# A layer-normalized RWKV attention with a Hadamard feed-forward: a recurrence with fewer VectorE passes, an earlier normalization, and one more quarter product split into seven

## The chip, the cores and the metric

The kernel runs on one core of a Trainium2 chip. The metric is the time of one execution on the device, in microseconds (us). Five engines of the core work side by side, each through its own instructions in order: TensorE (PE in the profile; PEld are its weight loads), VectorE (DVE), ScalarE (ACT), GpSimd (POOL) and SyncE (SP), which here issues nearly all transfers. An engine that waits for another one holds up everything that is queued behind the waiting instruction.

## The reference, cut to what matters

The input x has 4 sequences of 2048 tokens with 512 channels. H is 2048 in the feed-forward.

```python
xn = (x - mean) / sqrt(var + 1e-5)            # over the channels
shifted = xn one token later, zero first
xr, xk, xv = mu * xn + (1 - mu) * shifted     # one mu each
r, k, v = xr @ Wr.T, xk @ Wk.T, xv @ Wv.T
# recurrence over the tokens, per channel; w_eff = -exp(w)
#   p  = max(pp, u + k);      e1  = exp(pp - p);          e2  = exp(u + k - p)
#   y  = (e1 * aa + e2 * v) / (e1 * bb + e2)
#   p2 = max(w_eff + pp, k);  e1b = exp(w_eff + pp - p2); e2b = exp(k - p2)
#   aa, bb, pp = e1b * aa + e2b * v, e1b * bb + e2b, p2
att = (sigmoid(r) * y) @ Wo.T
hidden = silu(xn @ W1.T) * (xn @ W3.T)
ffn = fwht(hidden) @ W2.T                     # Hadamard transform of size 2048, scaled
out = x + att + ffn
```

All is in 32-bit floats. Of two numbers a and b, max(a, b) can be had as b + relu(a - b), and exp(a - max(a, b)) as exp(-relu(b - a)).

## The kernel before

**Blocks and stages.** The tokens are taken in eight blocks of 1024 (i from 0 to 7, two a sequence). Each block has two big stages on TensorE. In the first stage it makes k, v and r (projections; `projected_pair`, L429, six units, from block 1 on) and the hidden units (`up`, L459, sixteen units j = 0 to 15). From block 1 on the order is unit j = 0, the six projections (two of k, two of v, two of r), then j = 1 to 15. In the second stage (`down`, L747; `down_whole`, L655, for block 0) one last product gives attention and feed-forward together: the Hadamard transform is folded into W2 in block 0, and Wo is stacked to it.

**Seven products for eight.** A unit (`seven`, L371) multiplies 2 x 2 quarters by seven products instead of eight. Its TensorE order is fixed: forms 0, 4, 5, then the left-over work of the unit before (`tail`), then forms 1, 3, 6, 2. Between them ScalarE copies partial sums from one PSUM bank to another, so that a later product adds onto them:

```python
product(pa, 0, m11, True)
act.copy(pb, pa)
product(pf, 4, f1, True)
act.copy(s5, pf)
product(pb, 5, f2, False)
```

The third product of a unit therefore starts only after the copy `pb <- pa` is done. After form 3 come `on22` and after form 6 `on12`, where VectorE finishes two quarters and then `step()` (or `hook()`) issues one piece of other work.

**The recurrence.** `wkv(h)` (L287) does one of four channel groups ("heads" here) of the recurrence as whole-row instructions of 128 x 1024 on tiles `sa`, `sb`, `e1`, `e1b`, cut by `yield` into nine pieces. The first piece is a max-scan into `sa` and one subtraction into `sb`; the exponentials are on ScalarE. From block 1 on, head 0 is worked off during the projections at fixed calls of `hook()` (5, 6, 8, 11 to 15, 17; there are three in a projection: `on11`, `on22`, `on12`), so its first two pieces fall on `on22` and `on12` of the second projection. Before the piece each `hook()` also advances the mixing of xn with its shifted copy and its quarter differences (`mix_chores`). The other heads get two pieces a unit from j = 1 on: head 1 starts in `on22` of j = 1, head 2 in `on12` of j = 5, head 3 in `on22` of j = 10. In block 0 the pieces start at j = 0.

**Order.** All engines' instructions stand in the order of the program text (`InOrder`, L25, which is why nearly all rows of the profile name L35). Nothing is moved by a scheduler.

**The last product.** `down` splits the product by quarters again: seven forms (0 to 6). Forms 1 to 6 are split into seven a second time (`Deep`, L706), each a `step` of five matmul pairs of 256 columns; form 0, the one on the first quarters, is left plain: four steps of five matmul pairs of 512 columns (`plain_step`). Every 32-bit matmul shows as two records. `Deep.forms` are VectorE differences of 128 x 1280. Weight pieces of 320 KB come through a ring of eight slots (`pieces_w`), seven ahead of their use. `deep_forms` makes the weights of the second split once, on GpSimd, in block 1.

**Chores in `down`.** While the last product of a block runs, ScalarE takes mean and variance of the next block's tokens (`statistics`: 16 pieces on `x_tok`, which lies in `tf`), GpSimd the inverse root, SP writes both to memory and reads them back spread over all partitions (`spread`, in `v_sb`), and VectorE normalizes the next block's channels (`normalize`, eight instructions of 128 x 1024) and takes their four differences (`token_forms`).

Of the kernel before, what the change touches and what calls it, by code (L numbers as in the profile page):

```python
# [40 lines left out]
def tile_rwkv_attn_hadamard_ffn(  # L41
# [37 lines left out]
    down_w = dram.tile([2, 7, KH, P, QR, P], F32, name="down_w")  # L79
    deep_w = dram.tile([6, 7, P, QR, P], F32, name="deep_w")  # L80
    stat_d = dram.tile([n_blocks, 2, TB], F32, name="stat_d")


# [57 lines left out]
    def load_tokens(i):  # L141
        sp.dma_start(out=x_tok, in_=x[ds(i * TB, TB), :].rearrange("(p t) c -> p t c", p=P))

    def load_channels(i, t0=0, n=TB):
        dst = xnT[:, :, OFF + t0 : OFF + t0 + n]
        sp.dma_start(out=dst, in_=xT[:, ds(i * TB + t0, n)].rearrange("(b p) t -> p b t", p=P))

# [15 lines left out]
    def statistics(i):  # L163

        sums = small.tile([P, 2, TP], F32, tag="sums", name=f"sums_{i}")
        rs = small.tile([P, 2, TP], F32, tag="rs", name=f"rs_{i}")
        mean = small.tile([P, TP], F32, tag="mean", name=f"mean_{i}")
        for t in range(TP):
            tok = x_tok[:, t, :]
            act.activation(tok, tok, AF.Copy, accum_out=sums[:, 0, t : t + 1])  # L170
            yield
        pool.tensor_scalar(mean, sums[:, 0, :], -1.0 / C, None, ALU.mult)
        for t in range(TP):
            tok = x_tok[:, t, :]
            act.activation(tok, tok, AF.Square, bias=mean[:, t : t + 1], accum_out=sums[:, 1, t : t + 1])
            if t + 1 < TP:
                yield
        pool.tensor_scalar(rs[:, 0, :], sums[:, 1, :], 1.0 / C, EPS, ALU.mult, ALU.add)
        pool.tensor_tensor(rs[:, 0, :], rs[:, 0, :], neg_half, ALU.pow)
        pool.tensor_tensor(rs[:, 1, :], mean, rs[:, 0, :], ALU.mult)  # L180
        sp.dma_start(out=stat_d[i].rearrange("s (p t) -> p s t", p=P), in_=rs)
        sp.dma_start(out=spread, in_=stat_d[i].unsqueeze(0).to_broadcast([P, 2, TB]))
        yield

    def token_before(i):
# [5 lines left out]
    def normalize():  # L191

        for b in range(NB):
            for s, op in ((0, ALU.mult), (1, ALU.add)):
                xb = xnT[:, b, OFF : OFF + TB]
                dve.tensor_tensor(xb, xb, spread[:, s, :], op)
                yield

# [87 lines left out]

    def wkv(h):  # L287
        w_h, u_h = weff[:, h : h + 1], vec[:, 4, h : h + 1]
# [4 lines left out]
        cy = [carry[:, h, n : n + 1] for n in range(3)]  # L293

        def exp(t):
            act.activation(t, t, AF.Exp)


        copy(first_a, cy[0])
        scan(a1, w_h.to_broadcast([P, TB]), k, first_a, ALU.add, ALU.max)  # L300
        tt(b1, k, a1, ALU.subtract)
        yield
        stt(e1b, a0, w_h, a1, ALU.add, ALU.subtract)
        stt(e1, k, u_h, a0, ALU.add, ALU.max)
        stt(k, k, u_h, e1, ALU.add, ALU.subtract)
        tt(e1, a0, e1, ALU.subtract)
        copy(cy[0], last_a)
        yield
        exp(b1)
        exp(e1b)  # L310
        yield

        copy(first_a, cy[1])
        tt(a1, b1, v, ALU.mult)
# [4 lines left out]
        exp(e1)  # L319
        yield  # L320
        copy(first_b, cy[2])
        scan(b1, e1b, b1, first_b, ALU.mult, ALU.add)
        copy(cy[2], last_b)
        tt(v, k, v, ALU.mult)
        yield
        num, den = e1, e1b
        tt(den, e1, b0, ALU.mult)
        tt(den, den, k, ALU.add)
        dve.reciprocal(den[:, 0:H], den[:, 0:H])
        yield  # L330
# [217 lines left out]
    PARTS = ((0, 0), (1, 0), (1, 1), (0, 1))  # L548
    DEEP = (1, 4, 6, 5, 2, 3)

# [13 lines left out]
    def plain(form):  # L564
        return [("plain", form, PARTS[n]) for n in (0, 1, 3, 2)]

    def deep(m, *which):
        return [("deep", m, n) for n in which]

    order = (0, 1, 4, 6, 5, 3, 2)  # L570
    whole_program = [p for form in order for p in plain(form)]
    p1 = plain(0)
    program = [p1[0], p1[1], *deep(0, 0, 1), p1[2], *deep(0, 2), p1[3], *deep(0, 3, 4, 5), *deep(1, 0), *deep(0, 6)]
    for m, *which in (
# [39 lines left out]
    class Down:  # L614
# [30 lines left out]

        def plain_step(self, form, g, rh, pts, y, start=False):
            self.product(("plain", form, (rh, g)), pts[g], quarter(*y, rh, whole), whole, start and rh == 0)

        def plain_product(self, form, pts, y, then, start=False):
            for g in range(KH):  # L650
                for rh in range(2):
                    self.plain_step(form, g, rh, pts, y, start)
                then(g)

    def down_whole(i, chores, next_parts):  # L655
# [8 lines left out]
        chores.start()  # L664
        chores.statistics(2 * TP)
        next_parts()
# [10 lines left out]
        for g in range(KH):  # L677
            add(x22[g], s5[g])
        chores.tokens(6)
        d.plain_product(6, pc, (1, 1), lambda g: None)  # L680
# [7 lines left out]
        d.residual(x21, 1, 0)  # L688
        chores.tokens(2)

        def c22(g):
            add(x22[g], pb[g])
            d.store(x22[g], 1, g, 1)

        d.plain_product(3, pb, (0, 1), c22)
        chores.tokens(4)
        chores.mix()
# [48 lines left out]

    def down(i, chores, next_parts, last):  # L747
        d = Down(i)
# [13 lines left out]
        s5 = [s[:, cols] for s in s5 for cols in (lo, hi)]  # L762
        d0 = Deep(d, 0, sets[0], y21, [*free, in_k[2]], s5[0])
        d1 = Deep(d, 1, sets[1], y11, [slot(v_flat), *in_k[0:2], in_tf[0]], s5[2])
        d2 = Deep(d, 2, sets[0], y22, [*free, in_tf[1]], s5[1])
# [21 lines left out]

        def first(g, rh):
            d.plain_step(0, g, rh, pa, (0, 0), True)

        def with_u2(g):
            for slots, mh, half in ((x12, 0, 1), (x22, 1, 1), (x21, 1, 0)):
                add(slots[g], u2_of[g])
                if slots is not x21:
                    d.store(slots[g], mh, g, half)

        d.residual(x11, 0, 0)
        d.residual(x12, 0, 1)
        d.residual(x22, 1, 1)
        d0.clear()  # L800
        d0.forms(0, 1, 2, 3)
        first(0, 0)
        first(0, 1)
        d1.clear()
        chores.start()
        add(x11[0], pa[0])
        d0.step(0, 1)
        first(1, 0)
        chores.statistics(4)
        t1(0, 1)  # L810
        d1.forms(0)
        d0.step(2)
        chores.statistics(2)
        t3(0, 1)
        first(1, 1)
        chores.statistics(4)
        add(x11[1], pa[1])
        for g in range(KH):
            act.copy(u2_of[g], pa[g])
        t1(2, 3)  # L820
        d1.forms(1)
        d0.step(3)
        chores.statistics(1)
        d0.step(4)
        chores.statistics(2)
        d0.onto(0, x11)
        d1.forms(2, 3)
        d0.step(5)
        chores.statistics(1)
        d1.step(0)  # L830
        d0.step(6)
        chores.statistics(1)
        t3(2, 3)
# [4 lines left out]
        d1.step(1)  # L838
        chores.statistics(1)
        d5.step(0)  # L840
# [17 lines left out]
        d2.step(1)  # L858
        chores.tokens(3)
        d5.step(2)  # L860
        d1.step(5)
        d2.step(2)
        chores.tokens(2)
        d5.step(3)
# [29 lines left out]
        d4.forms(2)  # L894
        chores.tokens(2)
        d3.step(4)
# [6 lines left out]
        d3.step(5)  # L903
        chores.tokens(5)
        d4.step(5)
# [46 lines left out]
    class Chores:  # L952


        def __init__(self, i):
            self.i = i
            self.of_statistics, self.of_tokens = statistics(i), chain(normalize(), token_forms(dve))

# [4 lines left out]

        def do(self, pieces, n):
            if self.i < n_blocks:
                for _ in range(n):
                    next(pieces)

        def statistics(self, n):
            self.do(self.of_statistics, n)  # L970

        def tokens(self, n):
            self.do(self.of_tokens, n)

# [5 lines left out]
    for i in range(n_blocks):  # L980
# [5 lines left out]

        pieces = (None for h in range(NB) for _ in wkv(h))

# [81 lines left out]
        for j in range(0 if i == 0 else 1, NF):  # L1070
            w = group(j if i == 0 else 3 * KH + j)
            if i == 0 and j <= NR:
                if j > 1:
                    keep_down()
                if j < NR:
                    t = down_parts(0) if j == 0 else t_next
                    keep_down = down_forms(j, folded, t)
                    if j == 0:
                        keep_down()
                    t_next = down_parts(j + 1) if j + 1 < NR else None  # L1080
            if i == 1 and j in (3, 5, 7, 9, 11, 13):
                keep_deep(j // 2 - 1, t)
# [5 lines left out]
            tail = up(i, j, w, tail, step)  # L1088
        for f in tail:
            f()  # L1090
        for _ in pieces:
            pass


        def next_parts():
            if not last:
                parts.extend(load_parts(i + 1, n) for n in order_of(i + 1)[:2])

        if not last:
            load_tokens(i + 1)  # L1100
        if i == 0:
            down_whole(i, Chores(i + 1), next_parts)
        else:
            down(i, Chores(i + 1), next_parts, last)

# [52 lines left out]
```

## Time and profile before

| what | us |
|---|---|
| median of 3 runs (3043.6 to 3043.85) | 3043.84 |
| the profiled execution, its own time | 3040.92 |
| its span, first to last instruction | 3039.1 |
| TensorE busy | 3024.6 (100%) |
| VectorE busy | 2470.7 (81%) |
| ScalarE busy | 1015.1 (33%) |
| GpSimd busy | 232.3 (8%) |
| transfers, share of 16 engines (largest queue) | 37.9% |

An engine's busy time is the union of its instructions. TensorE's instructions overlap and their ends are modelled, so its busy share alone doesn't say that it never waits; the distance from one matmul's start to the next does. In a row of the timeline the first number is the start, the second how long the merged instructions take, x the number of instructions, and in brackets is the idle time ahead of it with the engine that ended it. The mean granted clock of TensorE is 0.999 of full speed.

### The profile page before, as it was taken

Reading aid. Unit: us, or ns where it says so; the run is one execution under the profiler, and the core shown is the slowest. Engines: PE = TensorE matmul, PEld = TensorE weight load, DVE = VectorE, ACT = ScalarE, POOL = GpSimd, SP = SyncE. Lnnn points to the kernel's source line nnn. Section 1 sums busy time; section 2 is a strip of 40 time slices with the busy share of each in tenths; the row PEclk is TensorE's granted clock in tenths of the full one; section 3 lists DMA queues with packets and bytes.
Section 4 is the critical chain, followed back from the end, with each engine's and each line's share of the span. In section 5 each row is a group of like instructions: output and inputs, shape, how many; then the busy total and the mean of one; then the engine's idle time right before and its main releaser. Section 6 shows DMA issues by size and latency. Waiting matters only on the chain.

```text
span 3039.1 us, 24405 instructions
## 1 busy us (share of the span) xinstructions
PE 3024.6 (100%) x8492; PEld 1613.1 (53%) x8492; DVE 2470.7 (81%) x2579; ACT 1015.1 (33%) x1822; POOL 232.3 (8%) x192
## 2 busy tenths in 40 slices
PE   8999999999999999999999999999999999999999
PEld 3444444447644476444854448544485445844458
DVE  7798648897888888888887878789798887988877
ACT  4233124332243323433233332433324333143321
POOL 3263002320000000000000000000000000000000
PEclk9999999999999999999999999999999999999999
DMA  4264523666422263222632236322453224522234
GB/s 175 76 213 160 190 90 128 216 215 221 133 82 76 79 235 132 73 78 100 226 119 82 73 130 203 113 74 84 159 169 118 73 73 170 180 95 85 73 115 151
DMA packets 136058, 397.64 MB, mean 131 GB/s; under 512 B 14336, under 2 KB 32768, under 8 KB 133760
## 3 DMA queue, kind: packets, MB, share of 16 engines
q1 hardware_dynamic: 135648, 395.50, 37.9%
q8 instruction: 68, 1.11, 0.1%
q10 hardware_dynamic: 288, 0.59, 0.1%
q14 instruction: 54, 0.44, 0.0%
HBM read 336.08 MB, written 59.96 MB: 130 GB/s over the span
## 4 chain that ended last, share of the span: by engine, by line
PE 96%; DVE 2%; DMA 1%; POOL 0%; ACT 0%; issue 0%; POOLq 0%; SPq 0%; ACTq 0%; DVEq 0%
PE bank L35 96%; DMA pieces_w<-deep_w 1%; POOL rs L35 0%; DVE right L35 0%; DVE e1b L35 0%; DMA right<-w 0%; DVE e L35 0%; DVE v_sb L35 0%; DMA stat_d<-rs 0%; DVE sb L35 0%; DVE bank L35 0%; DVE sa L35 0%; ACT tf L35 0%; DVE xnT L35 0%; POOLq L1154 0%
## 5 line engine op out<-in xcount | busy, mean ns | idle before, releaser
L35 PE MATMUL bank<-tf,part 128*128 128x512 f32 x2048 | 941.5, 592 | 0.0
L35 ACT COPY bank<-bank 128x512 f32<-128x512 f32 (+1 forms) x638 | 337.1, 528 | 1413.7 <-PE bank L35 1383.2
L35 PE MATMUL bank<-right,pieces_w 128*128 128x256 f32 (+1 forms) x2928 | 789.3, 429 | 0.4 <-DMA pieces_w<-deep_w 0.2
L35 PE MATMUL bank<-xnT,part 128*128 128x512 f32 x1536 | 722.0, 592 | 0.7 <-DVE right L35 0.7
L35 PEld LDWEIGHTS bank<-right,pieces_w 128*128 128x128 f32 x2928 | 555.9, 190 | 227.2 <-issue 166.7
L35 PEld LDWEIGHTS bank<-tf,part 128*128 128x128 f32 x2048 | 389.1, 190 | 489.8 <-issue 461.6
L35 PEld LDWEIGHTS bank<-xnT,part 128*128 128x128 f32 x1536 | 291.6, 190 | 366.4 <-issue 358.9
L35 DVE TENSOR_TENSOR right<-right 128x1280 f32<-128x1280 f32 (+2 forms) x236 | 327.7, 1414 | 63.4 <-PE bank L35 62.4
L35 PE MATMUL bank<-right,part 128*128 128x512 f32 x840 | 369.6, 593 | 0.0
L35 DVE SCALAR_TENSOR_TENSOR right<-right,bank 128x512 f32<-128x512 f32 x256 | 174.5, 682 | 223.3 <-ACT right L35 223.1
L35 PEld LDWEIGHTS bank<-right,part 128*128 128x128 f32 x840 | 158.4, 190 | 203.2 <-issue 189.4
L35 ACT ACTIVATE right<-bank 128x512 f32<-128x512 f32 x308 | 184.6, 600 | 130.1 <-PE bank L35 111.0
L35 DVE RECIPROCAL e1b<-e1b 128x512 f32<-128x512 f32 x64 | 214.1, 3347 | 1.1
L35 DVE TENSOR_TENSOR bank<-bank,s 128x512 f32<-128x512 f32 x256 | 168.7, 690 | 37.3 <-ACT bank L35 23.7
L35 DVE TENSOR_TENSOR right<-right,bank 128x512 f32<-128x512 f32 x256 | 173.5, 678 | 11.5 <-PE bank L35 7.1
L35 POOL TENSOR_SCALAR mean<-sums 128x8 f32<-128x8 f32 x7 | 5.8, 835 | 1869.6 <-ACT tf L35 1869.6
L35 DVE SCALAR_TENSOR_TENSOR right<-xnT,vec,right 128x1024 f32<-128x1024 f32 x92 | 121.5, 1357 | 7.9 <-ACT right L35 7.9
L35 ACT COPY s<-bank 128x512 f32<-128x512 f32 x128 | 75.0, 586 | 145.4 <-PE bank L35 145.4
L35 POOL TENSOR_TENSOR part<-part 128x256 f32<-128x256 f32 x88 | 89.1, 1023 | 203.9 <-DMA part<-wpart 96.9
L35 ACT ACTIVATE right<-xnT,omm 128x1024 f32<-128x1024 f32 x92 | 100.3, 1141 | 12.3 <-PE bank L35 12.3
L35 PE MATMUL bank<-pieces_w,part 128*128 128x512 f32 x224 | 100.7, 592 | 0.0
L35 PE MATMUL bank<-k_sb,pieces_w 128*128 128x256 f32 x420 | 97.5, 379 | 0.0
(120 smaller groups left out, 2299.8 us busy)
## 6 DMA issues: line engine op xcount, KB each, us to landing
part<-part_w SPq DMA_DIRECT2D x148, 896.0 KB, 4.6
pieces_w<-deep_w SPq DMA_DIRECT2D x294, 320.0 KB, 3.1
pieces_w<-down_w SPq DMA_DIRECT2D x80, 320.0 KB, 5.5
part_w<-part SPq DMA_DIRECT2D x22, 896.0 KB, 6.0
tf<-x SPq DMA_DIRECT2D x7, 2048.0 KB, 8.1
xnT<-xT SPq DMA_DIRECT2D x7, 2048.0 KB, 10.0
deep_w<-pieces_w SPq DMA_DIRECT2D x6, 2240.0 KB, 9.3
v_sb<-xT SPq DMA_DIRECT2D x48, 256.0 KB, 8.2
```

The costliest lines, as they stand in the source:

```text
L35: return self.tc.keep_in_program_order(issue(*args, **kwargs))
```

## The change

Three things are changed.

- **Recurrence.** The maxima and subtractions ahead of the exponentials are replaced by one signed difference, its two one-sided parts (`Relu` with scale 1 or -1 on ScalarE) and exponentials with scale -1. Per head three VectorE passes go and four ScalarE passes come. The first two `Relu` are in the second piece and read what the first piece leaves in `sb`.
- **Normalization.** For blocks 3 to 7 the channels are normalized one block earlier, during the hidden units of the block before: `normalize_early` uses `pieces_w` as scratch, and the result goes through a buffer in memory (`xn_d`). The token statistics move one block earlier too; block 0's last product does two sets.
- **Last product.** From block 1 on, form 0 is split into seven as well (`d6`), its steps alternating with those of the split form of the next one (`d0`). Its weights are made in block 0 at j = 12 and kept at j = 14.

```diff
-    deep_w = dram.tile([6, 7, P, QR, P], F32, name="deep_w")
+    deep_w = dram.tile([7, 7, P, QR, P], F32, name="deep_w")
+    xn_d = dram.tile([C, TB], F32, name="xn_d")
...
+    def normalize_early(i):
+        flat = pieces_w.rearrange("p u q c -> p (u q c)")
+        both = flat[:, 0 : 2 * TB].rearrange("p (s t) -> p s t", t=TB)
+        slots = [flat[:, ds((2 + n) * TB, TB)] for n in range(3)]
+        def load(b):
+            sp.dma_start(out=slots[b % 3], in_=xT[ts(b, P), ds(i * TB, TB)])
+        load_spread(i, both)
+        for b in range(3):
+            load(b)
+        yield
+        for b in range(NB):
+            xb = slots[b % 3]
+            for s, op in ((0, ALU.mult), (1, ALU.add)):
+                dve.tensor_tensor(xb, xb, both[:, s, :], op)
+                if s:
+                    sp.dma_start(out=xn_d[ts(b, P), :], in_=xb)
+                    if b + 3 < NB:
+                        load(b + 3)
+                yield
...
-    def wkv(h):
+    def wkv(h, ahead):
+        def below(out, t, sign):
+            act.activation(out, t, AF.Relu, scale=-sign)
         def exp(t):
-            act.activation(t, t, AF.Exp)
+            act.activation(t, t, AF.Exp, scale=-1.0)
         scan(a1, w_h.to_broadcast([P, TB]), k, first_a, ALU.add, ALU.max)
-        tt(b1, k, a1, ALU.subtract)
-        yield
-        stt(e1b, a0, w_h, a1, ALU.add, ALU.subtract)
-        stt(e1, k, u_h, a0, ALU.add, ALU.max)
-        stt(k, k, u_h, e1, ALU.add, ALU.subtract)
-        tt(e1, a0, e1, ALU.subtract)
+        stt(b1, a0, w_h, k, ALU.add, ALU.subtract)
         copy(cy[0], last_a)
         yield
+        below(e1b, b1, 1.0)
+        below(b1, b1, -1.0)
+        stt(e1, k, u_h, a0, ALU.add, ALU.subtract)
+        ahead(1)
+        yield
+        exp(e1b)
         exp(b1)
-        exp(e1b)
+        ahead(2)
         yield
+        below(k, e1, 1.0)
+        below(e1, e1, -1.0)
...
-    DEEP = (1, 4, 6, 5, 2, 3)
+    DEEP = (1, 4, 6, 5, 2, 3, 0)
...
-    program = [p1[0], p1[1], *deep(0, 0, 1), p1[2], *deep(0, 2), p1[3], *deep(0, 3, 4, 5), *deep(1, 0), *deep(0, 6)]
+    program = [p for n in (0, 4, 1, 2, 3, 5) for p in (*deep(6, n), *deep(0, n))]
+    program += [*deep(1, 0), *deep(6, 6), *deep(0, 6)]
...
+        d6 = Deep(d, 6, (*pa, sets[1][2]), y11, [*in_k, in_k[1]], s5[3])
...
-        d0.forms(0, 1, 2, 3)
-        first(0, 0)
-        first(0, 1)
...
+        d6.step(0)
+        d6.clear("f")
+        d0.clear("f")
+        d6.forms(0)
+        d0.step(0)
+        d0.forms(0)
+        d6.step(4)
+        d6.forms(1)
...
+            if j == 1:
+                ahead(1)
+            if i == 0 and j == NR + 2:
+                t = deep_forms(6)
+            if i == 0 and j == NR + 4:
+                keep_deep(6, t)
```

More of the change, by code (lines that the diff above doesn't have):

```diff
@@ L142, in load_tokens @@
         sp.dma_start(out=x_tok, in_=x[ds(i * TB, TB), :].rearrange("(p t) c -> p t c", p=P))
+    FIRST_EARLY = 3
     def load_channels(i, t0=0, n=TB):
         dst = xnT[:, :, OFF + t0 : OFF + t0 + n]
+        if i >= FIRST_EARLY:
+            sp.dma_start(out=dst, in_=xn_d.rearrange("(b p) t -> p b t", p=P))
+            return
         sp.dma_start(out=dst, in_=xT[:, ds(i * TB + t0, n)].rearrange("(b p) t -> p b t", p=P))
@@ L181, in statistics, with load_spread @@
         sp.dma_start(out=stat_d[i].rearrange("s (p t) -> p s t", p=P), in_=rs)
-        sp.dma_start(out=spread, in_=stat_d[i].unsqueeze(0).to_broadcast([P, 2, TB]))
         yield
+    def load_spread(i, out):
+        sp.dma_start(out=out, in_=stat_d[i].unsqueeze(0).to_broadcast([P, 2, TB]))
     def token_before(i):
@@ L319, in wkv @@
         exp(e1)
-        yield
         copy(first_b, cy[2])
@@ L323, in wkv @@
         copy(cy[2], last_b)
-        tt(v, k, v, ALU.mult)
         yield
         num, den = e1, e1b
+        tt(v, k, v, ALU.mult)
         tt(den, e1, b0, ALU.mult)
         tt(den, den, k, ALU.add)
+        yield
         dve.reciprocal(den[:, 0:H], den[:, 0:H])
@@ L571, in tile_rwkv_attn_hadamard_ffn @@
     whole_program = [p for form in order for p in plain(form)]
-    p1 = plain(0)
-    program = [p1[0], p1[1], *deep(0, 0, 1), p1[2], *deep(0, 2), p1[3], *deep(0, 3, 4, 5), *deep(1, 0), *deep(0, 6)]
+    program = [p for n in (0, 4, 1, 2, 3, 5) for p in (*deep(6, n), *deep(0, n))]
+    program += [*deep(1, 0), *deep(6, 6), *deep(0, 6)]
     for m, *which in (
@@ L644, in matmuls @@
                 )
-        def plain_step(self, form, g, rh, pts, y, start=False):
-            self.product(("plain", form, (rh, g)), pts[g], quarter(*y, rh, whole), whole, start and rh == 0)
         def plain_product(self, form, pts, y, then, start=False):
@@ L651, in plain_product @@
                 for rh in range(2):
-                    self.plain_step(form, g, rh, pts, y, start)
+                    rows = quarter(*y, rh, whole)
+                    self.product(("plain", form, (rh, g)), pts[g], rows, whole, start and rh == 0)
                 then(g)
@@ L664, in down_whole @@
         chores.start()
-        chores.statistics(2 * TP)
+        chores.statistics(2 * TP + 1)
         next_parts()
@@ L678, in down_whole @@
             add(x22[g], s5[g])
-        chores.tokens(6)
+        chores.normalize(6)
+        chores.statistics(1)
         d.plain_product(6, pc, (1, 1), lambda g: None)
@@ L688, in down_whole @@
         d.residual(x21, 1, 0)
-        chores.tokens(2)
+        chores.normalize(2)
+        chores.statistics(TP)
         def c22(g):
@@ L693, in c22 @@
             d.store(x22[g], 1, g, 1)
+        chores.statistics(TP - 1)
         d.plain_product(3, pb, (0, 1), c22)
-        chores.tokens(4)
+        chores.statistics(1)
+        chores.forms(4)
         chores.mix()
@@ L745, in onto, with down @@
                         dve.tensor_tensor(slot[g][:, hi], slot[g][:, hi], self.s5, ALU.add)
-    def down(i, chores, next_parts, last):
+    def down(i, chores, next_parts, last, before):
         d = Down(i)
@@ L762, in down @@
         s5 = [s[:, cols] for s in s5 for cols in (lo, hi)]
-        d0 = Deep(d, 0, sets[0], y21, [*free, in_k[2]], s5[0])
-        d1 = Deep(d, 1, sets[1], y11, [slot(v_flat), *in_k[0:2], in_tf[0]], s5[2])
+        d6 = Deep(d, 6, (*pa, sets[1][2]), y11, [*in_k, in_k[1]], s5[3])
+        d0 = Deep(d, 0, sets[0], y21, [*free, free[1]], s5[0])
+        d1 = Deep(d, 1, sets[1], y11, [slot(v_flat), in_k[0], in_k[2], in_tf[0]], s5[2])
         d2 = Deep(d, 2, sets[0], y22, [*free, in_tf[1]], s5[1])
@@ L786, in t4, with first_u2 @@
             sums(y21, y21, y22, *which)
-        def first(g, rh):
-            d.plain_step(0, g, rh, pa, (0, 0), True)
+        def first_u2(g):
+            u, pt = u2_of[g], (d6.a, d6.b)[g]
+            act.copy(u[:, lo], pt[:, lo])
+            dve.tensor_tensor(u[:, hi], pt[:, hi], d6.s5, ALU.add)
+            add(x11[g], u)
         def with_u2(g):
@@ L795, in with_u2 @@
                     d.store(slots[g], mh, g, half)
-        d.residual(x11, 0, 0)
-        d.residual(x12, 0, 1)
-        d.residual(x22, 1, 1)
-        d0.clear()
-        d0.forms(0, 1, 2, 3)
-        first(0, 0)
-        first(0, 1)
[L804 to L822, printed above, removed]
+        d6.clear("a")
+        d0.clear("a")
+        before()
+        d6.step(0)
[6 more added lines that the diff above has]
+        d6.forms(1)
+        d.residual(x11, 0, 0)
+        d0.step(4)
+        d0.forms(1)
+        d6.step(1)
+        d6.forms(2)
+        d0.step(1)
+        chores.statistics(2)
+        d6.step(2)
+        d6.forms(3)
+        d0.forms(2)
+        chores.statistics(2)
+        d0.step(2)
+        d0.forms(3)
+        t1(0)
+        chores.statistics(2)
+        d6.step(3)
+        t1(1)
+        chores.statistics(2)
+        d0.step(3)
+        d1.forms(0)
+        first_u2(0)
+        d1.clear()
+        chores.statistics(2)
+        d6.step(5)
+        t1(2, 3)
+        d.residual(x12, 0, 1)
         chores.statistics(1)
-        d0.step(4)
-        chores.statistics(2)
+        d0.step(5)
         d0.onto(0, x11)
-        d1.forms(2, 3)
-        d0.step(5)
         chores.statistics(1)
         d1.step(0)
+        d1.forms(1)
+        d.residual(x22, 1, 1)
+        chores.statistics(1)
+        d6.step(6)
+        t3(0, 1)
+        chores.statistics(1)
         d0.step(6)
-        chores.statistics(1)
+        chores.start()
+        d1.forms(2, 3)
+        first_u2(1)
         t3(2, 3)
@@ L838, in down @@
         d1.step(1)
-        chores.statistics(1)
+        chores.statistics(3)
         d5.step(0)
@@ L858, in down @@
         d2.step(1)
-        chores.tokens(3)
+        chores.normalize(3)
         d5.step(2)
@@ L862, in down @@
         d2.step(2)
-        chores.tokens(2)
+        chores.normalize(2)
         d5.step(3)
@@ L894, in down @@
         d4.forms(2)
-        chores.tokens(2)
+        chores.normalize(2)
         d3.step(4)
@@ L903, in down @@
         d3.step(5)
-        chores.tokens(5)
+        chores.normalize(1)
+        chores.forms(4)
         d4.step(5)
@@ L956, in __init__, with all_statistics @@
             self.i = i
-            self.of_statistics, self.of_tokens = statistics(i), chain(normalize(), token_forms(dve))
+            self.of_statistics = self.all_statistics()
+            self.of_normalize = iter(()) if i >= FIRST_EARLY else normalize()
+            self.of_forms = token_forms(dve) if i < n_blocks else iter(())
+        def all_statistics(self):
+            if self.i == 1:
+                yield from statistics(1)
+                load_spread(1, spread)
+                load_tokens(2)
+                yield
+            if self.i + 1 < n_blocks:
+                yield from statistics(self.i + 1)
+            if self.i == 2:
+                load_spread(2, spread)
+                yield
         def start(self):
@@ L962, in start, with normalize, forms @@
                 load_channels(self.i)
[L964 to L967, printed above, removed]
         def statistics(self, n):
-            self.do(self.of_statistics, n)
-        def tokens(self, n):
-            self.do(self.of_tokens, n)
+            for _ in range(n):
+                next(self.of_statistics, None)
+        def normalize(self, n):
+            for _ in range(n):
+                next(self.of_normalize, None)
+        def forms(self, n):
+            for _ in range(n):
+                next(self.of_forms, None)
         def mix(self):
@@ L984, in tile_rwkv_attn_hadamard_ffn, with ahead @@
             dve.memset(carry[:, :, 1:3], 0.0)
-        pieces = (None for h in range(NB) for _ in wkv(h))
+        early = normalize_early(i + 1) if FIRST_EARLY <= i + 1 < n_blocks else None
+        def ahead(n):
+            for _ in range(n if early else 0):
+                next(early, None)
+        pieces = (None for h in range(NB) for _ in wkv(h, ahead if h else lambda n: None))
         def step():
@@ L1088, in tile_rwkv_attn_hadamard_ffn, with before @@
             tail = up(i, j, w, tail, step)
[L1089 to L1092, printed above, removed]
+        def before():
+            for f in tail:
+                f()
+            for _ in pieces:
+                pass
+            if i == 0:
+                load_tokens(1)
+            elif i + 2 < n_blocks:
+                load_tokens(i + 2)
         def next_parts():
@@ L1097, in next_parts @@
                 parts.extend(load_parts(i + 1, n) for n in order_of(i + 1)[:2])
-        if not last:
-            load_tokens(i + 1)
         if i == 0:
+            before()
             down_whole(i, Chores(i + 1), next_parts)
         else:
-            down(i, Chores(i + 1), next_parts, last)
+            down(i, Chores(i + 1), next_parts, last, before)
 def kernel(**inputs):
```

## The prediction

> **What bounds the kernel now.** I read the page first: its busy times and its chain of waits.
>
> ```profile
> PE 3024.6 (100%) x8492; PEld 1613.1 (53%) x8492; DVE 2470.7 (81%) x2579; ACT 1015.1 (33%) x1822; POOL 232.3 (8%) x192
> PE 96%; DVE 2%; DMA 1%; POOL 0%; ACT 0%; issue 0%; POOLq 0%; SPq 0%; ACTq 0%; DVEq 0%
> ```
>
> TensorE is the bound, with no slack: matmul records outside the split forms start every 0.43 us, and after the first 23 us the starts fall behind that spacing by 2.4 us in all (1.25 in block 1, behind VectorE; 1.15 in three later blocks, where weight pieces queue on SP behind the statistics' store). So the time changes by TensorE work saved, less every new stall. VectorE's and ScalarE's busy times matter only where TensorE waits for them.
>
> **The split of form 0.** TensorE's timeline, block 0's unsplit last product and then split steps in block 4 (start, duration, x records):
>
> ```profile
> 305.90 120.33 PE L35 MATMUL bank<-right,pieces_w 128*128 128x512 f32 x280
> 1850.39 13.11 PE L35 MATMUL bank<-right,pieces_w 128*128 128x256 f32 x60
> 1863.35 2.32 PE L35 MATMUL bank<-tf,pieces_w 128*128 128x256 f32 x10
> ```
>
> The row after the first starts at 426.06: a 512-column record costs 120.16/280 = 0.429 us. From the other two, a 256-column one costs 12.96/60 = 0.216. Plain form 0 is 20 matmuls, 40 records, 17.17 us; split it is 7 x 5 matmuls, 70 records, 15.12. Saved: 2.05 a block, **14.3 us** in blocks 1 to 7. Making its weights lies on GpSimd, busy 8%: nothing.
>
> In exchange VectorE must make the forms of `d6` and `d0` early. Laid on the step times with 1.41 us for a 128 x 1280 subtraction, its queue is latest at the third difference of the third split form: ready 38.4 us into the stage, needed after 18 steps of 2.158, at 38.84. That fits with 0.4 us, because in blocks 2 to 6 the normalization no longer stands in `down`; everything else there has over 2 us. Below that margin it costs nothing, beyond it the lateness itself: 0 to 1.5 us a block; I take 0, the rows' own arithmetic.
>
> **Fewer VectorE passes, statistics earlier.** Three passes of some 1.3 us less a head, and 8 of 1.22 moved into the hidden units: VectorE isn't the bound there, so no gain. The moved loads (channels, spread) and stores (`xn_d`) are issued in unit j = 1 and used some 15 us later; like rows land in 5.4 us (spread) and 8.2 (256 KB of channels), so I take 0 (0 to 1 a block). The same 2 MB of channels then come from `xn_d` instead of x. Where the statistics' store no longer waits ahead of weight pieces, 1.15 us of stalls go, and block 1's 1.25 goes with the lighter VectorE: **2.4 us** gained (0 to 2.4).
>
> Block 0 takes two sets of statistics. The second 2 MB load enters SP's queue behind the spread, where four weight and mixing loads follow (340.8 to 342.9). The windows view shows 348 and 404 GB/s moved there already, so 2 MB take about 5.1 us, and the twelfth weight piece, landed at 349.3 and needed at 353.1, comes 1.3 late: **1.3 us** lost (0 to 3).
>
> **The first two `Relu`.** This decides. In `wkv`'s second piece ScalarE must wait for `sb`, which VectorE's first piece makes directly before. In ScalarE's order both `Relu` stand ahead of the next projection's copy `pb <- pa`, and that copy releases form 5 on TensorE. Head 0, block 4, timelines of VectorE, ScalarE and TensorE:
>
> ```profile
> 1580.45 2.35 DVE L35 TENSOR_TENSOR_SCAN sa<-weff,sa,k_sb 128x1024 f32<-128x1024 f32 x1
> 1582.90 1.23 DVE L35 TENSOR_TENSOR sb<-k_sb,sa 128x1024 f32<-128x1024 f32 x1
> ```
> ```profile
> 1583.06 0.57 ACT L35 COPY bank<-bank 128x512 f32<-128x512 f32 x1 [4.63 <-PE bank L35]
> ```
> ```profile
> 1582.81 3.60 PE L35 MATMUL bank<-pieces_w,part 128*128 128x512 f32 x8
> 1586.24 4.03 PE L35 MATMUL bank<-right,part 128*128 128x512 f32 x9
> ```
>
> The copy ran at 1583.06, as soon as form 0 was done. The TensorE row at 1582.81 is form 4 (four records) and then form 5, so form 5 starts at 1582.81 + 4 x 0.429 = 1584.53. After the change `sb` is a two-input pass with a scalar (1.28 instead of 1.23) and ready at about 1584.2. No row shows `Relu`. The nearest, exponentials of the same size on ScalarE:
>
> ```profile
> L35 ACT ACTIVATE sb<-sb 128x1024 f32<-128x1024 f32 x32 | 33.8, 1056 | 0.0
> ```
>
> Two of these end at 1586.3 (scaled copies of 1.14: 1586.5). The copy ends 0.57 later, and form 5 starts at 1586.9 instead of 1584.5: TensorE stands for **2.35 us** (2.2 to 2.6), once a block from block 1 on, 7 x 2.35 = **16.5** (15.4 to 18.2). Nothing makes it up, since TensorE has no slack.
>
> The same pair stands in the hidden units for heads 1 to 3. In blocks 2 to 7 head 1's first piece starts early enough: `Relu` and copy are over at 1644.5, needed at 1644.7, a margin of 0.2; I take 0 (0 to 0.5 each). In block 1 GpSimd makes the split weights, and VectorE's same instructions take longer beside it:
>
> ```profile
> 519.17 3.20 DVE L35 TENSOR_TENSOR_SCAN sa<-weff,sa,k_sb 128x1024 f32<-128x1024 f32 x1
> 522.40 2.38 DVE L35 TENSOR_TENSOR sb<-k_sb,sa 128x1024 f32<-128x1024 f32 x1
> ```
>
> That is 2.0 us later than in block 4, less the 0.2: **1.85** for head 1. Head 3, with a margin of 0.4, loses about **1.2** (0 to 2), and block 0's head 2 **0.2**.
>
> The Trainium skill ("ScalarE: Activation LUTs", "Rules for kernel authors") says that relu belongs on VectorE. By time alone the rows here disagree: 1.06 on ScalarE for 128 x 1024 in 32 bits, 1.22 to 1.28 on VectorE.
>
> **The sum without the clock.** 16.5 + 1.85 + 1.2 + 1.3 + 0.2 = 21.0 lost, 14.3 + 2.4 = 16.7 won: +4.3 us.
>
> **The clock.** The one long wait for VectorE in the trace, 2.76 us ahead of the matmul at 19.36, was followed by a halved clock; a shorter one at the end was not. Windows (length, busy time of PE, then of other engines; after POOL the granted clock):
>
> ```profile
> 15.50:18.90 3.40, 1.10 (x3) 0.19 (x1) 2.92 (x5) 0.96 (x3) 0.00 (x0) 1.00 1.03 386
> 18.90:22.30 3.40, 2.94 (x4) 1.39 (x5) 3.33 (x6) 1.22 (x2) 0.00 (x0) 0.51 1.05 395
> 3033.00:3036.30 3.30, 2.32 (x11) 1.71 (x9) 3.23 (x7) 0.00 (x0) 0.00 (x0) 1.00 0.47 179
> 3036.30:3039.10 2.80, 0.00 (x0) 0.00 (x0) 0.08 (x1) 0.00 (x0) 0.00 (x0) 1.00 0.47 163
> ```
>
> So a window with 32% of busy time was followed by half the clock, one with 70% was not. A stall of 2.35 us leaves 31% of such a window busy if it lies inside, and about 65% if it is cut in two. With the limit anywhere between 32% and 70%, about 5 of the 7 stalls fall below it, and each then costs half a window, 1.7 us: **+8.5** (0 to 7 x 1.7 = 11.9).
>
> By the Trainium skill ("TensorE: Matmul & The Clock Gate", "HAM oscillation") only idle gaps over about 3.4 us throttle again. The gap of 2.76 us above did, so I go by the row; by the page's rule the clock would stay and the time be 8.5 us less.
>
> **The sum.** 4.3 + 8.5 = +12.8 us. The profiled execution took 3040.92, so the changed one gives 3053.7. The median of the runs lies 2.92 above the profiled execution; I keep that: **3056.5 us**.
>
> **Rivals.**
> - *The stalls come, the clock holds.* For it: no gap after the start is longer than 0.73 us, so nothing shows what 2.35 does. The sum is +4.3 (2 to 7.5): 3048.1, or 3046 to 3051.
> - *The wait is covered* (the other side: not slower). If the first two `Relu` were done by the time form 4 ends, the 16.5 + 3.25 of the `Relu` and the clock's loss are away, and -16.7 + 1.3 = -15.4 is left; less 7 x 0.5 for thin margins, about -12: 3031.8 (3028 to 3036). It decides only if `sb` is ready 2.35 us earlier, by about 1581.85. VectorE's idle time of 5.2 us ahead of 1578.46 speaks for it, but that wait is for TensorE's products, from which the scan's `k` comes; scan and subtraction alone are 3.6 us. Also possible if the sums of TensorE's rows hide slack that I don't see.
> - *More than the stalls.* `Relu` takes turns with `Exp` eight times a block; one table load stands in the trace, at 1.28 us. If each turn loaded, 5 us of ScalarE a block would partly stretch the stalls, or `down`'s margin of 0.4 is missed by 1 to 2 us a block: +20 to +36, 3064 to 3080. Against it: the one load in the whole trace although exponentials and other functions already alternate.
>
> **How the numbers follow.** Clock falls: 0.50 (+8 to +20, 3051 to 3064). Clock holds: 0.28. Covered: 0.13. More than the stalls: 0.09. A measurement of this kernel can tell about 0.2% from no change, 6.1 us: "same" runs from 3037.8 to 3049.9. About a third of the second case lies beyond it, 0.09, as do all of the first and the last: slower 0.50 + 0.09 + 0.09 = 0.68; same 0.19; faster 0.13. The range leaves out the covered case and the far end of the last: 3045 to 3066.
>
> **What the profile after would show.** Right: TensorE idle once a projection stage, some 2.3 us, released by a ScalarE copy behind two `sb` activations of about 1.05 us that wait for VectorE; 280 fewer 512-column records in `down` and 490 more of 256 columns; stages of `down` shorter by 2; granted clock below 1.0 in a window behind each stall. Wrong: no gap there, or the clock at 1.00 right behind it, or gaps in `down` released by VectorE.

## The result, and the profile after

| | median, us | executions | lowest to highest |
|---|---|---|---|
| before | 3043.6 | 5 | 3040.7 to 3043.85 |
| after | 3052.48 | 5 | 3051.91 to 3058.63 |

The changed kernel is slower: ratio 1.0038, 95% interval 1.0023 to 1.0052. The profiled execution took 3052.48 against 3040.92 before, 11.6 us more (spans 3050.7 and 3039.1); the forecast for it was 12.8 more. By medians the loss is 8.9, because three of the five executions of before lay near 3043.8, 2.9 above the profiled one.

The page of the kernel after, busy times and chain:

```profile
PE 3014.0 (99%) x8702; PEld 1653.5 (54%) x8702; DVE 2391.1 (78%) x2525; ACT 1153.9 (38%) x1992; POOL 213.7 (7%) x196
...
PE 95%; DVE 3%; ACT 1%; DMA 1%; issue 0%; POOL 0%; SPq 0%; DVEq 0%; ACTq 0%; POOLq 0%
```

TensorE has 10.6 us less to do and VectorE 80 us less, and yet the span is longer: TensorE now stands. ScalarE is in the chain with 1%, where it had 0%. The waits view of TensorE (wait, total us, times, longest) names the engine:

```profile
PE bank L35 <- ACT bank L35: 18.3, 8, 3.4
...
PE bank L35 <- POOL part L35: 2.3, 1, 2.3
PE bank L35 <- DMA pieces_w<-down_w: 1.6, 1, 1.6
```

None of these three stood there before. The 2.3 us that the view puts down to GpSimd are the same stall in block 1: the two `Relu` and the copy stand ahead of it there too, and in the runs without `Relu` on ScalarE (e4, e5, e7 below) TensorE never waits for GpSimd. The place is the predicted one. Head 0 in block 4, timelines of VectorE, ScalarE and TensorE:

```profile
1589.26 2.35 DVE L35 TENSOR_TENSOR_SCAN sa<-weff,sa,k_sb 128x1024 f32<-128x1024 f32 x1
1591.71 1.28 DVE L35 SCALAR_TENSOR_TENSOR sb<-sa,weff,k_sb 128x1024 f32<-128x1024 f32 x1
```
```profile
1593.03 1.06 ACT L35 ACTIVATE e1b<-sb 128x1024 f32<-128x1024 f32 x1 [5.80 <-DVE sb L35]
1594.12 1.06 ACT L35 ACTIVATE sb<-sb 128x1024 f32<-128x1024 f32 x1
1595.08 0.58 ACT L35 COPY bank<-bank 128x512 f32<-128x512 f32 x1
```
```profile
1591.62 1.88 PE L35 MATMUL bank<-pieces_w,part 128*128 128x512 f32 x4
1595.72 1.98 PE L35 MATMUL bank<-pieces_w,part 128*128 128x512 f32 x4 [2.22 <-ACT bank L35]
```

ScalarE sits idle for 5.8 us until `sb` is there, does the two `Relu` of 1.06, and only then the copy. Form 4's four records start at 1591.62 and are through at 1591.62 + 4 x 0.429 = 1593.34; form 5 starts at 1595.72, 2.38 us late (the bracket shows less because the ends of matmuls are modelled).

**Where the 11.6 us are.** From TensorE's starts: seven such stalls, 7 x 2.38 = 16.7; head 1 of block 1, 1.7; head 3 of block 1, 3.6; the weight piece in block 0, 1.7; three stretches of halved clock, 1.7 + 1.7 + 1.5 = 4.9 (the rows follow). Lost: 28.6. Won: the last product takes 105.76 instead of 107.82 (block 3), 7 x 2.06 = 14.4, the waits for `deep_w` pieces 1.2, and a stretch of halved clock in the first 25 us, 1.8, that only the profiled execution of before has. 28.6 - 17.4 = 11.2; smaller terms are left out.

**The clock.** Windows of the kernel after (length, busy time of PE, PEld, DVE, ACT, POOL, then the granted clock, the share of the DMA engines and GB/s):

```profile
1219.00:1222.40 3.40, 1.18 (x4) 0.68 (x4) 3.40 (x4) 2.68 (x4) 0.00 (x0) 0.99 0.10 42
1222.40:1225.80 3.40, 3.40 (x5) 1.33 (x4) 0.25 (x1) 1.07 (x2) 0.00 (x0) 0.50 0.00 0
1966.40:1969.80 3.40, 1.31 (x3) 0.68 (x4) 3.40 (x4) 2.52 (x4) 0.00 (x0) 1.00 0.07 27
1969.80:1973.20 3.40, 3.40 (x5) 1.33 (x4) 0.10 (x1) 1.07 (x2) 0.00 (x0) 0.51 0.00 0
2338.60:2342.00 3.40, 2.14 (x5) 0.59 (x4) 3.30 (x6) 1.69 (x2) 0.00 (x0) 1.00 0.64 240
2342.00:2345.40 3.40, 2.44 (x6) 1.25 (x7) 2.37 (x3) 1.84 (x4) 0.00 (x0) 1.00 0.00 0
```

The same stall of 2.38 us is followed by half the clock in blocks 3 and 5 and by nothing in block 6, nor in the other four. The third halved stretch follows the 3.6 us of block 1.

### The profile page after: what moved, and what is told of

Same layout as the page of the kernel before. It is cut to its first block, busy times and chain, and to the rows that moved or that the text cites. A ratio compares the mean times of both kernels' runs of the same rounds, so it can differ in the third digit from the quotient of the medians.

```text
span 3050.7 us, 24995 instructions
## 1 busy us (share of the span) xinstructions
PE 3014.0 (99%) x8702; PEld 1653.5 (54%) x8702; DVE 2391.1 (78%) x2525; ACT 1153.9 (38%) x1992; POOL 213.7 (7%) x196
## 4 chain that ended last, share of the span: by engine, by line
PE 95%; DVE 3%; ACT 1%; DMA 1%; issue 0%; POOL 0%; SPq 0%; DVEq 0%; ACTq 0%; POOLq 0%
PE bank L35 95%; DVE sa L35 1%; DVE e1b L35 0%; DVE right L35 0%; DMA pieces_w<-down_w 0%; DVE sb L35 0%; ACT tf L35 0%; ACT bank L35 0%; ACT e1b L35 0%; ACT sb L35 0%; DVE pieces_w L35 0%; DMA right<-w 0%; DVE v_sb L35 0%; DMA part<-wpart 0%; DVE e L35 0%
## 5 line engine op out<-in xcount | busy, mean ns | idle before, releaser
L35 ACT COPY bank<-bank 128x512 f32<-128x512 f32 (+1 forms) x659 | 344.8, 523 | 1195.5 <-PE bank L35 1167.2
L35 PE MATMUL bank<-right,pieces_w 128*128 128x256 f32 (+1 forms) x2928 | 733.5, 409 | 1.6 <-DMA pieces_w<-down_w 1.6
L35 PE MATMUL bank<-k_sb,pieces_w 128*128 128x256 f32 x630 | 146.3, 379 | 0.0
L35 PEld LDWEIGHTS bank<-k_sb,pieces_w 128*128 128x128 f32 x630 | 119.7, 190 | 16.3
```

The source lines that it names most:

```text
L35: return self.tc.keep_in_program_order(issue(*args, **kwargs))
```

## The experiments

Behind each time stands in brackets its ratio to before, with the 95% interval. The median of before was 3041.67 beside e1 to e4, 3042.11 beside e5, e6, e7 and e9, and 3043.06 beside e8 and e11.

### The same two `Relu`, one hook later (e1_hook7)

```diff
-                    if hooks[0] in (5, 6, 8, 11, 12, 13, 14, 15, 17):
+                    if hooks[0] in (5, 7, 8, 11, 12, 13, 14, 15, 17):
```

> The changed kernel with one number altered: head 0's second piece, with the first two Relu, is issued at hook 7 instead of hook 6, behind the next projection's first copy instead of ahead of it. Theory (ScalarE's in-order queue makes the seven stalls of 2.38 us): all seven go, 7 x 2.38 = 16.7, and with them the two halvings of the clock that follow such a stall in the profile (2 x 1.7): 3052.5 - 20 = about 3032. The stalls of block 1 (1.7 and 3.6) and of block 0 (1.7) stay. Rival (the four added ScalarE passes a head, or VectorE's new order, cost the time wherever they stand): the stalls only move, 3047 to 3053.

Measured: 3045.07 (ratio 1.0015, 1.0006 to 1.0024). A miss by 13: the stalls moved. ScalarE and TensorE in block 4:

```profile
1593.07 2.19 ACT L35 ACTIVATE right<-xnT,omm 128x1024 f32<-128x1024 f32 x2
1595.16 1.04 ACT L35 ACTIVATE e1b<-sb 128x1024 f32<-128x1024 f32 x1
1596.23 1.06 ACT L35 ACTIVATE sb<-sb 128x1024 f32<-128x1024 f32 x1
1597.19 0.58 ACT L35 COPY bank<-bank 128x512 f32<-128x512 f32 x1
```
```profile
1590.67 5.31 PE L35 MATMUL bank<-right,part 128*128 128x512 f32 x12
1597.83 3.70 PE L35 MATMUL bank<-right,part 128*128 128x512 f32 x8 [1.85 <-ACT bank L35]
```

At hook 7 ScalarE waits for nothing, but the two mixing passes of the hook and the two `Relu` fill the 4.1 us ahead of the copy after form 3 (1593.07 to 1597.19). TensorE should go on at 1590.67 + 12 x 0.429 = 1595.82 and does at 1597.83: 2.01 late, in each of the seven blocks. None of these is followed by a halved clock. So my theory was too narrow: the wait for `sb` isn't the point; ScalarE work ahead of a copy that TensorE is about to need costs whatever it makes that copy late, with or without a wait of ScalarE's own.

### One `Relu` instead of two ahead of the copy (e2_one_relu)

```diff
         below(e1b, b1, 1.0)
-        below(b1, b1, -1.0)
         stt(e1, k, u_h, a0, ALU.add, ALU.subtract)
         ahead(1)
         yield
+        below(b1, b1, -1.0)
         exp(e1b)
```

> The changed kernel with one of the first two Relu moved to the third piece, in all heads. Theory: each stall of 2.38 becomes 2.38 - 1.06 = 1.3 us, 7 x 1.06 = 7.4 less; block 1's two stalls become 0.7 and 2.5, 2.1 less; and a stall of 1.3 is too short to halve the clock, which takes 3.4 to 5 off: 3052.5 - 13 to 14.5 = about 3039. If the halvings have nothing to do with the length of the stall: 3043.

Measured: 3041.79, like before (ratio 1.0, 0.999 to 1.0009). The seven stalls are 1.29 to 1.34, block 1's two 0.67 and 2.50, as expected. No window behind a stall of 1.3 shows a lower clock. Of the 2.8 us above the expectation, about 2 are a halved clock in the first 25 us of the profiled execution, which the kernel after doesn't have in its own.

### Two more `Relu` ahead of the copy (e3_four_relu)

```diff
-        below(e1b, b1, 1.0)
+        for _ in range(3 if h == 0 else 1):
+            below(e1b, b1, 1.0)
         below(b1, b1, -1.0)
```

> The changed kernel with head 0's first Relu issued three times (the same result), so four passes stand ahead of the copy. Theory: the stalls grow by 2 x 1.06 to 4.5 us, 7 x 2.1 = 14.8 more. A stall of 4.5 covers over 2.1 us of some stretch of 3.4 us wherever such stretches begin, so the clock is halved behind each of the seven, not behind two: 5 x 1.7 = 8.4 more, 3052.5 + 23 = about 3075.7. If a halving comes by chance or from something else than the idle time: 3052.5 + 14.8 = 3067.

Measured: 3081.66 (ratio 1.0134, 1.0117 to 1.015). The stalls are 4.56 to 4.61, and now each of the seven is followed by a lower clock. Two of the windows (columns as above):

```profile
859.80:863.20 3.40, 3.40 (x5) 1.35 (x4) 0.00 (x0) 0.30 (x1) 0.00 (x0) 0.50 0.00 0
...
1614.00:1617.40 3.40, 3.40 (x5) 1.33 (x5) 0.00 (x0) 0.88 (x2) 0.00 (x0) 0.50 0.00 0
```

The halved stretches are up to twice as long as I counted: the granted clock stays at half for 3.4 us behind three of the seven stalls and for 6.8 us behind four, and 1.4 to 3.1 us are lost behind each, some 3.7 more in all than I counted. The rest of the 6 us by which the time lies above the expectation is a longer halved stretch behind block 1's long stall (1.6 more) and a new stall of 1.7 in block 0, whose head 0 has the four `Relu` as well. Together the two runs show that the halving goes with the length of the stall: 1.3 never, 2.4 sometimes, 4.6 always.

### The one-sided parts on VectorE (e4_relu_dve)

```diff
-            act.activation(out, t, AF.Relu, scale=-sign)
+            dve.tensor_scalar(out, t, -sign, 0.0, ALU.mult, ALU.max)
```

> The changed kernel with all four one-sided parts of a head on VectorE (multiply, then maximum with zero) instead of ScalarE; the rest stays. ScalarE then has nothing in the second piece that waits for sb. Theory: the seven stalls, block 1's two and the halvings go, 16.7 + 1.7 + 3.6 + 5 = 27, and 4 passes a head on VectorE, 1.2 us each or less, mostly lie beside TensorE: 3025.5 to 3029. Rival (VectorE needs to be relieved, the three passes taken from it are what carries the split): stalls released by VectorE of 1 to 2 us a block, 3033 to 3040.

Measured: 3029.3 (ratio 0.9959, 0.9944 to 0.9974). TensorE waits for ScalarE nowhere, and the largest wait after the start is the weight piece of block 0:

```profile
PE bank L35 <- DMA right<-w: 7.5, 1, 7.5
PE bank L35 <- DVE tf L35: 2.8, 1, 2.8
PE bank L35 <- DMA pieces_w<-down_w: 2.8, 1, 2.8
PE bank L35 <- DVE right L35: 0.2, 1, 0.2
```

The four passes are cheap on VectorE (groups by line and form; busy us, mean ns):

```profile
L35 DVE TENSOR_SCALAR sb<-sb 128x1024 f32<-128x1024 f32 x32 | 25.9, 808 | 1.1
...
L35 DVE TENSOR_SCALAR e1b<-sb 128x1024 f32<-128x1024 f32 x32 | 23.1, 722 | 0.0
```

### The old recurrence in the changed kernel (e5_old_recurrence)

The body of `wkv` is that of the kernel before; all else stays.

> The changed kernel with the recurrence of the kernel before (maxima and subtractions on VectorE, no Relu); early normalization and the split of form 0 stay. Theory: the stalls of head 0, block 1's two and their halvings of the clock go, the 14.3 us of the split stay: 3052.5 - 27 = 3025.5 to 3030. Rival (VectorE needs the three passes taken off it to carry the split): new stalls released by VectorE of 1 to 2 us a block, 3033 to 3040.

Measured: 3028.25 (ratio 0.9957, 0.994 to 0.9974). With 122 us more of VectorE work than the kernel after (2513.5 busy), TensorE waits for VectorE 1.3 us in all. The three passes taken off VectorE weren't needed.

### The new recurrence alone in the kernel before (e6_new_recurrence_alone)

The body of `wkv` is that of the kernel after; all else is as before.

> The kernel before with the new recurrence alone (Relu on ScalarE), plain form 0, normalization where it was. Theory: the whole loss comes from here. Before, 3041.7 here, plus 7 x 2.38 = 16.7, plus 1.7 and 2.3 in block 1, plus 3 to 5 for halved clocks: 3065 to 3068. Rival (part of the loss comes from the split's or the early normalization's new order on VectorE or SP): less than 3060.

Measured: 3066.77 (ratio 1.0085, 1.007 to 1.01). The stalls are the same, with the split and without it:

```profile
PE bank L35 <- ACT bank L35: 18.5, 8, 3.4
...
PE bank L35 <- POOL part L35: 2.3, 1, 2.3
```

The profiled execution has half the clock behind one of its seven stalls, in block 3.

### The split alone (e7_split_alone), and all but the early normalization (e8_no_early)

Both normalize all blocks in the last product; the first has the old recurrence as well.

```diff
-    FIRST_EARLY = 3
+    FIRST_EARLY = n_blocks
...
                 yield from statistics(self.i + 1)
-            if self.i == 2:
-                load_spread(2, spread)
+            else:
+                yield from range(2 * TP)
+            if 2 <= self.i < FIRST_EARLY:
+                load_spread(self.i, spread)
                 yield
```

> Form 0 split into seven, with the recurrence of the kernel before and all blocks normalized in the last product (the token statistics stay one block earlier). Theory that the split's VectorE work fits only just, with a margin of 0.4 us, because the normalization is out of the last product: of the 14.3 + 1.2 won, 7 x 1 to 2 is lost again to differences that come late, 3033 to 3041. If VectorE catches up (eight passes of 1.22 fit in its idle time): 3041.7 - 15.5 + 1.7 (block 0) = 3028.

Measured: 3025.8 (ratio 0.995, 0.9935 to 0.9965). My tight margin in `down` does not exist in the sense I gave it: with all eight normalization passes back, the last product still takes 105.76 us in blocks 1 to 6. TensorE's waits behind the first 20 us:

```profile
...
PE bank L35 <- DMA pieces_w<-down_w: 1.7, 1, 1.7
PE bank L35 <- DVE right L35: 0.7, 2, 0.5
```

The other one:

> The changed kernel with all blocks normalized in the last product, so without the early normalization; new recurrence and split stay. Theory (the loss is the Relu pair's alone, the early normalization neither costs nor brings anything that can be measured): 3052 within 5, for the halvings of the clock differ from execution to execution. Rival (the early loads and stores cost something, or the early place is what lets the split fit): a gain, or a loss, of 7 us and more.

Measured: 3055.37 (3048.92 to 3058.42; ratio 1.0046, 1.0029 to 1.0062). Its profiled execution has the same 2.38 in each block, and halved stretches behind it in blocks 1, 3 and 6, where the kernel after has them in 3 and 5. The run before and e5 also differ in the early normalization alone: 3025.8 without it, 3028.25 with it. It is worth nothing that these runs show.

### Block 0's second load of tokens later (e9_relu_dve_tokens, e11_split_tokens)

```diff
                 load_spread(1, spread)
+                yield
                 load_tokens(2)
                 yield
```

First with the one-sided parts on VectorE, then on the split alone.

> The changed kernel with the one-sided parts on VectorE, as in the run before, and in block 0 the second load of tokens issued one form later (12 to 17 us), behind the weight pieces that are due. Theory: the one stall left after the start, 2.9 us for a weight piece in block 0, goes, with the 1.3 us of halved clock behind it: 3029.3 - 4.2 = 3025. Rival (the load delays weight pieces wherever it stands): 3028 to 3030.

Measured: 3025.3 (ratio 0.9946, 0.9931 to 0.9961).

> The split of form 0 alone, with the recurrence of the kernel before and without early normalization, and in block 0 the second load of tokens issued one form later. Theory: the stall for a weight piece in block 0, 1.8 in the run before, goes: 3025.8 - 1.8 = 3024. Block 1's waits for VectorE (0.65 and 0.42) stay. Rival: the load delays weight pieces wherever it stands, or statistics that end later delay block 1: 3026 and more.

Measured: 3024.89 (3024.6 to 3025.08; ratio 0.9942, 0.9927 to 0.9957). TensorE's waits in the second, all of them:

```profile
PE bank L35 <- DMA right<-w: 7.5, 1, 7.5
PE bank L35 <- DVE tf L35: 2.8, 1, 2.8
PE bank L35 <- DVE right L35: 1.6, 2, 1.4
```

The wait for a weight piece is gone in both. The two first lines belong to the first 20 us; the third is in block 1, where VectorE runs beside GpSimd, and its first wait is longer than expected, 1.5 instead of 0.65. These two are the fastest versions by their medians, 0.5 to 0.6% under before, and can't be told apart from each other by these times, nor from the split alone (3025.8).

## Why the prediction was right, and where it was off

- **Direction and mechanism: right.** The `Relu` pair ahead of the copy was named with its place and price: 2.35 forecast, 2.38 measured, in seven blocks. The new recurrence alone costs 24.7 us (3066.77 - 3042.11; by the interval 21 to 30), the split with the earlier statistics wins 16.3 (3042.11 - 3025.8; 11 to 20): together +8.4, against +8.9 by the medians of before and after.
- **The split: right.** 2.05 a block forecast, 2.06 measured.
- **The clock: mechanism right, term too large.** I forecast five halvings of 1.7 behind the seven stalls, 8.5; the profiled execution has two, and a third behind block 1's long stall, 4.9 together. By the prediction's own signs (a lower clock behind each stall) this part failed in five of the seven blocks. What I missed is that the place of the stall counts as much as its length. The clock records of all twelve traces show a fixed grid: every stretch between two changes of the granted clock lasts a whole multiple of 3.413 us (here 744.1 us, 218 times, between the second halved stretch and the third), the halved ones 3.41 or 6.83. Here are the two closest cases, blocks 1 and 5, cut on that grid:

```profile
464.60:468.02 3.42, 1.42 (x4) 0.35 (x2) 3.42 (x5) 2.43 (x3) 0.98 (x2) 1.00 0.97 363
468.02:471.43 3.41, 3.14 (x8) 1.50 (x9) 2.63 (x2) 1.76 (x4) 3.33 (x3) 1.00 0.03 11
1966.47:1969.88 3.41, 1.39 (x3) 0.68 (x4) 3.41 (x3) 2.45 (x4) 0.00 (x0) 1.00 0.04 15
1969.88:1973.30 3.42, 3.42 (x6) 1.35 (x5) 0.02 (x1) 1.07 (x2) 0.00 (x0) 0.50 0.00 0
```

With TensorE busy for 1.42 us of the window the clock held, with 1.39 it fell. Every window of the twelve traces, from 12 us on, agrees: at full clock none with 1.42 us or more was followed by half the clock, and each with 1.39 or less was. So the limit lies near 41%, within the 32 to 70% of the prediction, and a stall that a grid line cuts well costs only its own length. How many of seven stalls of 2.38 fall below the limit differs with where they lie on the grid: two here, one in e6, three in e8. The longer executions of the kernel after, 3055.13 and 3058.63, were granted 0.997 of the clock on average and the three shorter ones 0.998, which fits more halvings; there is no trace of them.

- **The nearness of the number: in part luck.** For the profiled execution 12.8 more was forecast and 11.6 came, but single terms were further off and cancelled: the clock cost 3.6 less than forecast, and 1.8 us of halved clock at the start of before had no counterpart after; block 1's head 3 cost 2.4 more and block 0's load 0.4 more. The other 2.9 us between the forecast and 3052.48 come from the step to the median: that of before lay 2.92 above its profiled execution, that of after is its profiled execution. (3040.92 + 12.8 + 2.92 is 3056.6; the prediction has 3056.5.)
- **Block 1's head 3: under-priced.** 1.2 forecast, 3.6 measured. I added nothing for the two VectorE passes just ahead of the scan, which took 2.45 instead of 1.25 beside GpSimd, as the rows of before already showed (2.44). Head 1 was right: 1.85 and 1.7.
- **Block 0's load: right,** 1.3 forecast, 1.7 measured (1.3 to 2.9 in the other runs), and gone when the load is issued later.
- **The margin in `down`: wrong, without effect.** I held 0.4 us of margin to be there because the normalization had moved away. The split alone keeps the normalization and loses nothing there. The rival that put its price on this margin had no ground.
- **The 2.4 us of old stalls: half right.** The waits for weight pieces went; of block 1's 1.25 about 0.4 stayed.
- **The rule I set aside: wrong to do so.** The Trainium skill ("ScalarE: Activation LUTs", "Rules for kernel authors") puts relu on VectorE. I compared ScalarE's 1.06 us with VectorE's two-input passes of 1.22 to 1.28; the one-input pass takes 0.69 to 0.81. By the time of the pass too the rule holds here, and following it turns the kernel from 1.0038 to 0.9959 of before. What it won there was above all the place in the queue: nothing on ScalarE then stands ahead of the copy.
- **The clock rule.** The Trainium skill ("TensorE: Matmul & The Clock Gate", "HAM oscillation") warns of idle gaps over about 3.4 us. Here gaps of 2.38 were followed by half the clock in two places of seven, and gaps of 4.6 seven times out of seven; the shorter ones would not have counted by the page's rule.

## What to carry to other kernels

When an engine works in order and also does the small copies that feed the bottleneck, the question about any new instruction on it is what stands behind it in the queue and when the bottleneck needs that, not how busy the engine is: ScalarE was busy 38% of the time and cost 16.7 us. Take work from an engine only after asking whether the bottleneck waits for it: the 80 us saved on VectorE bought nothing, the 2 us a block saved on TensorE came off the time in full. Of a bundle of three edits, time each alone before keeping them together; here one of them was worth about 16 us, another cost about 25, and the third did nothing that could be measured.

## What the runs showed of the hardware

- The cost of a stall on TensorE isn't proportional to its length: 1.3 us costs 1.3, 2.4 costs 2.4 or 4.1 by where it falls, and 4.6 costs 6.0 to 7.7, because 3.4 or 6.8 us of half clock follow.
- The granted clock changes on a grid of 3.413 us, at places that differ from execution to execution. In all twelve traces a window of the grid at full clock in which TensorE is busy for 1.39 us or less is followed by a window at half the clock, one with 1.42 or more is not.
- The first wait for VectorE after the start, 2.8 us in all twelve profiles, was followed by half the clock in six of them (before, e1, e2, e4, e6, e9) and not in the other six; between before and after that makes 1.8 us: the same code in the same place. Part of the 3 to 4 us between executions of one kernel may come from this.
